# Where the experts of a graph network's last FFN are computed: inside the second attention's stream, or beside the weighted sum before it, with their outputs kept in DRAM

## The chip, the cores and the metric

One core of a Trainium2 chip runs the whole program. The metric is the device time of one execution in microseconds. A core has TensorE (PE in the profile, its weight loads are PEld), VectorE (DVE), ScalarE (ACT), GpSimd (POOL) and SyncE (SP), each with an instruction stream of its own that it executes in order; they wait for each other through semaphores. DMAs are issued from the streams of SP, ACT and POOL.

## What is computed

6250 nodes with 256 features go through four layers; each adds its output to x. `A` is the layer norm without parameters, the edge list has 206250 edges sorted by destination.

```python
x = x + gat(A(x), edges)               # attention of 4 heads x 64 over the edges
x = x + ffn0(A(x))                     # 8 experts, the best 2 per node
x = x + weighted(A(x), src, dst, w)    # sum of w * neighbour, two 256x256 matmuls, unit norm
x = x + ffn1(A(x))                     # below
```

The last layer has its own graph of 131072 edges over 8192 numbers (a second attention), which gives only the gates; its FFN has four experts, 256 to 512 to 256, and the code computes all four for every node:

```python
h = (x @ W_gat)                                     # 4 heads x 4 experts
agg = segment softmax over the edges of h           # (attention as in gat), + b_gat
s = layernorm(agg).reshape(M, 4, 4).mean(1)         # scores of the experts
w = softmax(top2(s))                                # gates g: two of four are not zero
out = sum_e g[e] * (gelu(x @ W1[e] + b1[e]) @ W2[e] + b2[e])
```

`x` inside the last layer is `A(x)` of the sum before it. The FFN's input is thus known as soon as the weighted layer has finished a node, and the gates only after the second attention.

## The kernel before

Nodes lie in 49 blocks of 128 (the last one has 106), one node per partition; X (all blocks) stays in SBUF. The edges are cut into tiles of 128, eight tiles make a piece (`Q`). Each of the three streams over edges (attention, weighted sum, second attention) works alike: GpSimd gathers the rows of the 128 sources of a tile with one indirect DMA from a table in DRAM; VectorE makes a one-hot matrix of the destinations (`one_hots`, L1092); PE multiplies it with the gathered rows and so sums them by destination in PSUM.

The program is written out in an order by hand (`manual_schedule`): Python loops over steps `s_`, and in each step emits the gathers of a piece that will be used later, and the later stages of pieces gathered in earlier steps. Every engine executes its share of that order.

**The weighted sum** (loop at L1867 to L1905, `fast`). There are 202 pieces (1612 gathers, helper at L233). In step `s_`: the gathers of piece `s_` into a tile `g1` with six buffers; the matmuls of piece `s_ - 3` (L1885), at the end of a window the copy `kept` (L1888); then the steps of a chain that a finished block goes through, one per step: `move` (L1810), `side` (transposes), `dense` (L1827 to L1832, two matmuls of 256x256 into `po`, bias, leaky ReLU), `norm` (square and square root on ACT, L1838, L1839, the addition to X, L1842), `next_ln` (the last layer's norm), `next_h` (transposes, `xT` stored to `xt_d` in DRAM, the matmul with `W_gat` into `ph`, L1855), `next_rows` (a copy and two stores, L1860 to L1862: the table of the second attention); last, the scaling of piece `s_ - 2` by the edge weights on ACT (L1903) and its one-hots on DVE.

Ahead of this loop stand its loads and, after them, the layer norms of X that write the table `tab_ef`.

**The second attention** (`layer1_fast` and `gat_stream`) begins behind a branch on a flag (`tc.If`), when all of the weighted sum is done. It has 99 pieces (787 gathers from `tab_1f`, L1199, nine buffers). A step takes the gathers of piece `s_`, the scores of piece `s_ - 2` (a matmul L1220, its reduction `nd` L1229, additions to `Z`), the greatest score per destination for four pieces together (L1245 to L1271), the messages (L1278) cut into three bf16 parts (L1283, L1285), and the sums of piece `s_ - 7` (L1301). Five times in a step it calls `beside()`, which takes one item of the list `work`.

That list holds the FFN. When the four blocks of a group have been summed, `group` loads their `xT` (`xt`, 512 KB), computes the gates (`route`) and appends the work: for each expert four `inner` items (L1624: two matmuls of 128x128 by 512 nodes; GELU on ACT, L1629), four `outer` items (L1635: four matmuls by 256; the result times its gate is added to X on DVE, L1640), and `offsets` (L1614 to L1619: the gates times `b2`). PSUM gives two buffers `pf` to these items; what follows the matmuls of an item (GELU, addition) is emitted at the next call. After the group's last item its rows of X are stored to `out`. When the loop ends, `while beside()` empties the list.

Of the kernel before, what the change touches and what calls it, by code (L numbers as in the profile page):

```python
# [31 lines left out]
P = 128  # L32
LN_EPS = 1e-5
BIG = float(2**100)
CH = 7
# [35 lines left out]
def tile_kernel(ctx, tc, src_ins, out):  # L71
# [1450 lines left out]
    def layer1_fast(s1, si1, dl1, il1, ha_d, tab_1, xt_d):  # L1522
# [3 lines left out]
        W1 = D1 + H1  # L1526
        HD = I["L1_ffn_W1"].shape[2]
        FC = HD // P
        with tc.tile_pool(name="g1f", bufs=1) as g1, tc.tile_pool(name="f1w", bufs=2) as fp, \
                tc.tile_pool(name="f1_ps", bufs=2, space=PSUM) as fpp:  # L1530
# [13 lines left out]
            w1 = g1.tile([P, E1, KD, HD], F32, name="w1")  # L1544
            nc.scalar.dma_start(w1, I["L1_ffn_W1"].rearrange("e (k p) f -> p e k f", p=P))
            w2 = g1.tile([P, E1, FC, D], F32, name="w2")
            nc.scalar.dma_start(w2, I["L1_ffn_W2"].rearrange("e (c p) d -> p e c d", p=P))
            bt = g1.tile([P, E1, FC], F32, name="bt")
            with nc.allow_non_contiguous_dma(reason="biases along the partitions"):
                nc.scalar.dma_start(bt, I["L1_ffn_b1"].rearrange("e (c p) -> p e c", p=P))  # L1550
            b2 = g1.tile([E1, D], F32, name="b2")
            nc.scalar.dma_start(b2, I["L1_ffn_b2"])
# [4 lines left out]
            ag, work, gates, xts, hs, late = {}, [], {}, {}, {}, []  # L1557
# [4 lines left out]
            def load_x(g):  # L1562
                n = len(blocks_in(g)) * P
                xts[g] = fp.tile([P, KD, GB * P], F32, name="xt")
                nc.sync.dma_start(xts[g][:, :, :n], xt_d[:, :, g * GB * P:g * GB * P + n])
# [4 lines left out]
            def done(b, acc, hs_, mp):  # L1570
                a = mp.tile([P, D1 + 2 * H1], F32, name="a24")
                nc.vector.tensor_reduce(a, acc.rearrange("p s w -> p w s"), AX.X, OP.add)
                po = mp.tile([P, H1], F32, name="po")
                nc.scalar.activation(po, a[:, W1:], AF.Exp, scale=-1.0)  # L1574
                rd = mp.tile([P, H1], F32, name="rd")
                nc.vector.scalar_tensor_tensor(rd, a[:, D1:W1], 1e-16, po, op0=OP.add, op1=OP.add)
                nc.vector.reciprocal(rd, rd)

                def hd(x):
                    return x.rearrange("p (h c) -> p h c", h=H1)  # L1580

                g = b // GB
                if g not in ag:
                    ag[g] = fp.tile([P, GB, D1], F32, name="ag")
                o = mp.tile([P, D1], F32, name="o")
                nc.vector.tensor_mul(hd(o), hd(hs_), po[:, :, None].to_broadcast([P, H1, C1]))
                nc.vector.tensor_add(o, o, a[:, :D1])
                nc.vector.tensor_mul(hd(ag[g][:, b % GB, :]), hd(o), rd[:, :, None].to_broadcast([P, H1, C1]))
                if b == blocks_in(g)[-1]:
                    group(g)  # L1590

            def group(g):

                bl = blocks_in(g)
                n = len(bl)
                N_ = n * P
                load_x(g)
                gates[g] = route(fp, ag.pop(g), n, vec)
                for e in range(E1 + 1):
                    if e < E1:  # L1600
                        for f in range(FC):
                            work.append(lambda e=e, f=f: inner(g, e, f, N_))
                    else:
                        work.append(lambda: None)
                    if e == 0:
                        work.append(lambda: offsets(g))
                    else:
                        for j in range(n):
                            work.append(lambda e=e - 1, j=j: outer(g, e, j, e == E1 - 1 and j == n - 1))

            def offsets(g):
                for j, b in enumerate(blocks_in(g)):
                    pg = fpp.tile([P, 512], F32, name="pf")
                    nc.tensor.transpose(pg[:E1, :P], gates[g][:, j, :], ident)  # L1614
                    gt = fp.tile([E1, P], F32, name="gt")
                    nc.scalar.copy(gt, pg[:E1, :P])
                    pb = fpp.tile([P, 512], F32, name="pf")
                    nc.tensor.matmul(pb[:, :D], gt, b2, start=True, stop=True)  # L1618
                    nc.vector.tensor_add(X[:, b, :], X[:, b, :], pb[:, :D])  # L1619

            def inner(g, e, f, n):
                ph = fpp.tile([P, 512], F32, name="pf")
                for k in range(KD):
                    nc.tensor.matmul(ph[:, :n], w1[:, e, k, f * P:(f + 1) * P], xts[g][:, k, :n],  # L1624
                                     start=(k == 0), stop=(k == KD - 1))

                def gelu():
                    h = hs[g, e, f] = fp.tile([P, 512], F32, name="h", bufs=2 * FC)
                    nc.scalar.activation(h[:, :n], ph[:, :n], AF.Gelu, bias=bt[:, e, f:f + 1])  # L1629
                late.append(gelu)  # L1630

            def outer(g, e, j, last):
                py = fpp.tile([P, 512], F32, name="pf")
                for f in range(FC):
                    nc.tensor.matmul(py[:, :D], hs[g, e, f][:, j * P:(j + 1) * P], w2[:, e, f, :],  # L1635
                                     start=(f == 0), stop=(f == FC - 1))
                b = g * GB + j

                def put():
                    nc.vector.scalar_tensor_tensor(X[:, b, :], py[:, :D], gates[g][:, j, e:e + 1], X[:, b, :],  # L1640
                                                   op0=OP.mult, op1=OP.add)
                    if last:
                        store(g)
                late.append(put)
# [9 lines left out]
            def beside():  # L1654
                todo = late[:]
                late.clear()
                if work:
                    work.pop(0)()
                for f in todo:
                    f()  # L1660
                return bool(work or late)
# [5 lines left out]
    def fast(flag_s0, last_d, dl_d):  # L1667
# [105 lines left out]
        xt_d = dram.tile([P, KD, NP], F32, name="xt_df")  # L1773
        with tc.tile_pool(name="n1f", bufs=1) as ep, tc.tile_pool(name="n1fw", bufs=2) as mp, \
                tc.tile_pool(name="n1f_ps", bufs=1, space=PSUM) as pp:
# [10 lines left out]
            for t0, n in chunks(NT, CH):  # L1786
                em = mp.tile([P, CH, D], F32, name="em")
                layernorm(mp, em, X[:, t0:t0 + n, :], n)
                nc.sync.dma_start(tab_e[t0 * P:(t0 + n) * P].rearrange("(t p) d -> p t d", p=P), em[:, :n])
            wg = layer1_weights(ep)  # L1790
            ips = place_iota(pp)
# [32 lines left out]
            def dense(b, eT, sT):  # L1824
                po = pp.tile([P, D], F32, name="po")
                for k in range(KD):
                    nc.tensor.matmul(po, eT[:, k], w12[:, 0, k], start=(k == 0), stop=False)  # L1827
                for k in range(KD):
                    nc.tensor.matmul(po, sT[:, k], w12[:, 1, k], start=False, stop=(k == KD - 1))
                o = mp.tile([P, D], F32, name="on")  # L1830
                nc.vector.tensor_add(o, po, bias)  # L1831
                nc.vector.scalar_tensor_tensor(o, o, 0.2, o, op0=OP.mult, op1=OP.max)  # L1832
                return o

            def norm(b, o):
                sq = mp.tile([P, D], F32, name="sq")
# [12 lines left out]
            def next_h(b, xl):  # L1849
                xT = mp.tile([P, KD, P], F32, name="xT1")  # L1850
                transposed(pp, xT, xl[:, 0, :])
                nc.sync.dma_start(xt_d[:, :, b * P:(b + 1) * P], xT)
                ph = pp.tile([P, D1 + 2 * H1], F32, name="ph1")
                for k in range(KD):
                    nc.tensor.matmul(ph, xT[:, k], wg[:, k], start=(k == 0), stop=(k == KD - 1))  # L1855
                return ph

            def next_rows(b, ph):
# [3 lines left out]
                nc.sync.dma_start(ha_d[:, b, :], h)  # L1862

            chain = {side: dense, dense: norm, norm: next_ln, next_ln: next_h, next_h: next_rows}


            with tc.manual_schedule():  # L1867
                after = {}
                s_ = 0
                while s_ < npiece + 3 or any(k >= s_ for k in after):  # L1870
                    if s_ < npiece:
                        t0, n = span(s_)
                        g = piece[s_] = mp.tile([P, Q, D], F32, name="g1", bufs=6)
# [3 lines left out]
                    if 0 <= q < npiece:  # L1877
                        t0, n = span(q)
                        g = piece.pop(q)
                        for b, a, m, oh in hots.pop(q):  # L1880
# [3 lines left out]
                            for t in range(a, a + m):  # L1884
                                nc.tensor.matmul(acc[b], oh[:, t - a], g[:, t - t0, :], start=(t == lo), stop=(t == hi))  # L1885
                            if hi == a + m - 1:
# [13 lines left out]
                    if 0 <= k < npiece:  # L1900
# [4 lines left out]
                        hots[k] = one_hots(s0, k, mp, ips, dl, 4)  # L1905
                    s_ += 1
        keep.close()
        v1 = nc.values_load(flag1[0:1, 0:1], min_val=0, max_val=1,
                            skip_runtime_bounds_check_because="a comparison: 0 or 1")
        with tc.If(v1 == 1) as cmp1:  # L1910
            layer1_fast(s1, si1, dl1, il1, ha_d, tab_1, xt_d)
# [46 lines left out]
```

## Time and profile before

| | |
|---|---|
| time, three runs | 7729.37 us median (7711.49 to 7736.43) |
| the profiled execution | 7741.2 us, span 7739.3 us |
| busy: PE / DVE / ACT / POOL | 4514.6 / 3064.3 / 1496.6 / 4066.3 us |
| TensorE's granted clock, mean | 0.773 |
| gathers of the first attention | 205 to 2535 us |
| ffn0 and the sort of the second edge list | about 2540 to 3690 us |
| gathers of the weighted sum | 3737 to 6068 us |
| gathers of the second attention | 6126 to 7555 us |
| HBM traffic | 720 MB read, 57 MB written |

The page gives each engine's busy time, then forty slices of the span with a digit for the busy share of each engine and for TensorE's granted clock, then groups of instructions by line. "x1612 | 1525.6, 946 | 907.7 <-issue" means: 1612 instructions, 1525.6 us busy, 946 ns each, 907.7 us of idle time of the engine just before them, most of it ended by its own issuing. "remote" as a releaser is a semaphore update for which the profile shows no finished instruction at that time. PE's ends are modelled. Further views that the prediction uses: busy time of each engine in chosen stretches, waits (who waited for whom, total us, times, longest), and instructions in order of time (start, us, engine, line, operation, in brackets the idle time before it and its releaser).

Three rows of the page's slices (each slice 193.5 us, digits in tenths):

```profile
PE   3355545554555679997255555555555426667668
...
POOL 0666666666666012321466666666666554555550
PEclk9677777777777689998577777777777658888888
```

### The profile page before, as it was taken

To read this page: it belongs to the slowest core of one execution; us is meant where nothing else is said; L and a number is where in the kernel's file an instruction comes from. 1 tells how busy PE (TensorE), PEld (TensorE's weight loads), DVE (VectorE), ACT (ScalarE), POOL (GpSimd) and SP (SyncE) were. 2 spreads that over 40 slices of the span, in tenths; PEclk is the share of its full clock that TensorE was granted. 3 is DMA by queue.
4 is the path that set the end of the run, shared out by engine and by line. 5 is a ranking of instruction groups with operands and counts; after the bars stand their busy time and mean duration, and the time that the engine had idled before them with its cause. 6 is when DMAs were issued, how large, how long until landed. Compare 5 with 4: busy or idle time off the path is not lost. (4 is left out here: it accounts for less than half of the span.)

```text
span 7739.3 us, 63529 instructions
## 1 busy us (share of the span) xinstructions
PE 4514.6 (58%) x19991; PEld 3428.3 (44%) x19991; DVE 3064.3 (40%) x7283; ACT 1496.6 (19%) x3742; POOL 4066.3 (53%) x4308
## 2 busy tenths in 40 slices
PE   3355545554555679997255555555555426667668
PEld 2233333433343558886144444444444314444445
DVE  4354545554544762442311211111111245555554
ACT  2000000000000112222133333333333201222222
POOL 0666666666666012321466666666666554555550
PEclk9677777777777689998577777777777658888888
DMA  4444444444444145565333333333333311111110
GB/s 132 125 120 119 121 118 118 120 120 117 120 121 118 45 131 186 188 220 173 114 92 98 99 97 97 95 96 99 96 93 98 89 28 31 36 36 31 37 36 11
DMA packets 483566, 778.20 MB, mean 101 GB/s; under 512 B 146575, under 2 KB 307759, under 8 KB 483186
## 3 DMA queue, kind: packets, MB, share of 16 engines
q0 software_dynamic: 190688, 461.74, 22.7%
q1 hardware_dynamic: 279998, 301.12, 12.9%
q10 hardware_dynamic: 12532, 11.16, 0.5%
q8 instruction: 162, 2.65, 0.1%
q14 instruction: 186, 1.52, 0.1%
HBM read 720.07 MB, written 56.78 MB: 100 GB/s over the span
## 5 line engine op out<-in xcount | busy, mean ns | idle before, releaser
L233 POOL DMA_INDIRECT g<-tab_ef,si x1612 | 1525.6, 946 | 907.7 <-issue 562.8
L1199 POOL DMA_INDIRECT g<-tab,si x1612 | 1538.7, 955 | 811.3 <-issue 516.6
L1885 PE MATMUL acc<-g,oh 128*128 128x256 f32 x3224 | 1013.5, 481 | 856.8 <-DVE oh L1092 565.8
L1885 PEld LDWEIGHTS acc<-g,oh 128*128 128x128 f32 x3224 | 784.9, 249 | 1059.1 <-ACT g L1903 574.4
L1199 POOL DMA_INDIRECT g<-tab_1f,si1s x787 | 750.5, 954 | 681.6 <-issue 570.7
L1301 PE MATMUL acc<-g,oh 128*128 128x264 f32 x3224 | 942.7, 452 | 109.4 <-DVE g L1278 60.3
L1301 PEld LDWEIGHTS acc<-g,oh 128*128 128x128 f32 x3224 | 720.9, 230 | 302.3 <-DVE g L1278 99.7
L1903 ACT ACTIVATE g<-g,wt 128x256 f32<-128x256 f32 x1612 | 663.9, 495 | 57.6 <-DMA g<-tab_ef,si 53.2
L1327 PE MATMUL bacc<-kept,wide 128*128 128x264 f32 x400 | 200.5, 652 | 648.4 <-ACT kept L1314 602.1
L1624 PE MATMUL pf<-xt,w 128*128 128x512 f32 (+1 forms) x832 | 449.1, 681 | 143.7 <-DMA xt<-xt_df 66.7
L1635 PE MATMUL pf<-w,h 128*128 128x256 f32 x1568 | 412.5, 415 | 155.5 <-DVE X L1640 103.9
L1092 DVE TENSOR_TENSOR oh<-ips,dl 128x1024 f32<-128x1024 f32 x404 | 489.1, 1211 | 0.0
L1278 DVE TENSOR_TENSOR g<-g,pe 128x2048 f32<-128x2048 f32 (+2 forms) x301 | 486.5, 1616 | 0.0
L1229 DVE TENSOR_REDUCE nd<-pd 128x64 f32<-128x192 f32 (+1 forms) x301 | 106.6, 354 | 907.8 <-remote 464.1
L1888 DVE COPY kept<-acc 128x256 f32<-128x256 f32 x101 | 42.9, 425 | 1014.9 <-remote 581.0
L1327 PEld LDWEIGHTS bacc<-kept,wide 128*128 128x128 f32 x400 | 110.7, 305 | 677.6 <-ACT kept L1314 611.3
L1635 PEld LDWEIGHTS pf<-w,h 128*128 128x128 f32 x1568 | 310.4, 206 | 220.4 <-DVE X L1640 113.7
L600 PE MATMUL ph<-xe,w 128*128 128x256 f32 x1792 | 400.9, 381 | 0.0
L613 PE MATMUL py<-w,h 128*128 128x256 f32 x1792 | 399.0, 380 | 0.0
L1831 DVE TENSOR_TENSOR on<-po,bias 128x256 f32<-128x256 f32 x49 | 20.8, 424 | 911.4 <-remote 850.9
L600 PEld LDWEIGHTS ph<-xe,w 128*128 128x128 f32 x1792 | 339.8, 191 | 45.3
L613 PEld LDWEIGHTS py<-w,h 128*128 128x128 f32 x1792 | 337.1, 191 | 43.4
(465 smaller groups left out, 5077.4 us busy)
## 6 DMA issues: line engine op xcount, KB each, us to landing
w<-in_L_ffn_W SPq DMA_DIRECT2D x112, 1024.0 KB
db<-s_d SPq DMA_DIRECT2D x299, 256.0 KB
g<-tab,si POOLq DMA_INDIRECT x1612
g<-tab_ef,si POOLq DMA_INDIRECT x1612
g<-tab_1f,si1s POOLq DMA_INDIRECT x787
yy<-tab_y SPq DMA_DIRECT2D x7, 1792.0 KB
kf<-s_keep SPq DMA_DIRECT2D x76, 96.2 KB
bb<-in_L_ffn_b SPq DMA_DIRECT2D x56, 128.0 KB
```

The costliest lines, as they stand in the source:

```text
L233: nc.gpsimd.indirect_dma_start(out=dst, out_offset=None, in_=table, in_offset=bass.IndirectOffsetOnAxis(ap=si[:, t:t + 1], axis=0))
L600: nc.tensor.matmul(ph, w1[:, k, f * P:(f + 1) * P], xe[:, k, :], start=(k == 0), stop=(k == KD - 1))
L613: nc.tensor.matmul(py, hs[f][:, i * P:(i + 1) * P], w2[:, f, :], start=(f == 0), stop=(f == FC - 1))
L1092: nc.vector.tensor_tensor(o[:, :m], ips[:, None, k * P:(k + 1) * P].to_broadcast([P, m, P]), dl[:, a:a + m, None].to_broadcast([P, m, P]), ...
L1199: nc.gpsimd.indirect_dma_start(out=g[:, j, :DH + H], out_offset=None, in_=tab, in_offset=bass.IndirectOffsetOnAxis(ap=si[:, t0 + j:t0 + j ...
L1278: nc.vector.tensor_mul(gh, gh, ps[i][:, o:o + n, :, None].to_broadcast([P, n, H, CD]))
L1301: nc.tensor.matmul(acc[b].rearrange("p s w -> p (s w)"), oh[:, t - a], m_, start=(t == lo), stop=(t == hi))
L1327: nc.tensor.matmul(sums_of[b].rearrange("p s w -> p (s w)"), shift_to(s, i, b), t, start=(i == of[0]), stop=(i == of[-1]))
L1624: nc.tensor.matmul(ph[:, :n], w1[:, e, k, f * P:(f + 1) * P], xts[g][:, k, :n], start=(k == 0), stop=(k == KD - 1))
L1635: nc.tensor.matmul(py[:, :D], hs[g, e, f][:, j * P:(j + 1) * P], w2[:, e, f, :], start=(f == 0), stop=(f == FC - 1))
L1885: nc.tensor.matmul(acc[b], oh[:, t - a], g[:, t - t0, :], start=(t == lo), stop=(t == hi))
L1903: nc.scalar.activation(piece[k][:, j, :], piece[k][:, j, :], AF.Copy, scale=wt[:, t0 + j:t0 + j + 1])
```

## The change

The FFN is taken out of the second attention and put beside the weighted sum. A new function `dense_ffn` holds its weights and its items; the weighted sum calls `beside()` behind the matmuls 1, 4 and 7 of each piece, and empties the list after its loop. `next_h` writes the transposed rows straight into the group's tile `xt` and starts a group's items when its last block has come; `xt_d` is gone. An `outer` item no longer knows a gate: DVE adds `b2` (now broadcast over the partitions) and the 128x256 result of one block and one expert goes to a new DRAM tensor `y_d` (196 stores of 128 KB). In the second attention `done` loads the four outputs of its block (`yb`, 512 KB, five buffers), and `group`'s list holds one item per block: four additions of gate times output to X on DVE. `offsets` and the FFN's weights are gone from there.

So that all of it fits: `g1` has five buffers (six before), the one-hots three (four), `sq` one (two), `po` and `ph` share the PSUM tile of the transposes, and `next_rows` is part of `next_h`. The layer norms that write `tab_ef` now stand ahead of the stream's loads, in a pool of their own.

```diff
+    def dense_ffn(e_pool, fp, fpp, y_d):
...
+        def start(g):
+            bl = range(g * GB, min(NT, (g + 1) * GB))
+            n = len(bl)
+            for e in range(E1 + 1):
+                for f in range(FC):
+                    if f == FC // 2 and e > 0:
+                        for j in range(n):
+                            work.append(lambda e=e - 1, j=j: outer(g, e, j))
+                    if e < E1:
+                        work.append(lambda e=e, f=f: inner(g, e, f, n * P))
+                    elif f < FC // 2:
+                        work.append(lambda: None)
+
+        def inner(g, e, f, n):
+            ph = fpp.tile([P, 512], F32, name="pf")
+            for k in range(KD):
+                nc.tensor.matmul(ph[:, :n], w1[:, e, k, f * P:(f + 1) * P], xts[g][:, k, :n],
+                                 start=(k == 0), stop=(k == KD - 1))
+
+            def gelu():
+                h = hs[g, e, f] = fp.tile([P, 512], F32, name="h", bufs=FC + FC // 2)
+                nc.scalar.activation(h[:, :n], ph[:, :n], AF.Gelu, bias=bt[:, e, f:f + 1])
+            late.append(gelu)
+
+        def outer(g, e, j):
+            py = fpp.tile([P, 512], F32, name="pf")
+            for f in range(FC):
+                nc.tensor.matmul(py[:, :D], hs[g, e, f][:, j * P:(j + 1) * P], w2[:, e, f, :],
+                                 start=(f == 0), stop=(f == FC - 1))
+
+            def put():
+                y = fp.tile([P, D], F32, name="y1", bufs=2)
+                nc.vector.tensor_add(y, py[:, :D], b2[:, e])
+                nc.sync.dma_start(y_d[g * GB + j, :, e, :], y)
+            late.append(put)
+
+        def beside():
+            todo = late[:]
+            late.clear()
+            if work:
+                work.pop(0)()
+            for f in todo:
+                f()
+            return bool(work or late)
...
+            def load_y(b):
+                if b < NT:
+                    ys[b] = fp.tile([P, E1, D], F32, name="yb", bufs=GB + 1)
+                    nc.sync.dma_start(ys[b], y_d[b])
...
+                load_y(b)
                 g = b // GB
...
+            def put(gates, j, b):
+                y = ys.pop(b)
+                for e in range(E1):
+                    nc.vector.scalar_tensor_tensor(X[:, b, :], y[:, e, :], gates[:, j, e:e + 1], X[:, b, :],
                                                    op0=OP.mult, op1=OP.add)
...
-                po = pp.tile([P, D], F32, name="po")
+                po = pp.tile([P, KD, P], F32, name="pt").rearrange("p k e -> p (k e)")
...
-                xT = mp.tile([P, KD, P], F32, name="xT1")
+                o = b % GB * P
+                xT = room(b // GB)[:, :, o:o + P]
                 transposed(pp, xT, xl[:, 0, :])
-                nc.sync.dma_start(xt_d[:, :, b * P:(b + 1) * P], xT)
-                ph = pp.tile([P, D1 + 2 * H1], F32, name="ph1")
+                ph = pp.tile([P, KD, P], F32, name="pt")[:, 0, :D1 + 2 * H1]
...
+                if b % GB == GB - 1 or b == NT - 1:
+                    start(b // GB)
...
-                        g = piece[s_] = mp.tile([P, Q, D], F32, name="g1", bufs=6)
+                        g = piece[s_] = mp.tile([P, Q, D], F32, name="g1", bufs=5)
...
                                 nc.tensor.matmul(acc[b], oh[:, t - a], g[:, t - t0, :], start=(t == lo), stop=(t == hi))
+                                if t - t0 in (1, 4, 7):
+                                    beside()
...
-                        hots[k] = one_hots(s0, k, mp, ips, dl, 4)
+                        hots[k] = one_hots(s0, k, mp, ips, dl, 3)
                     s_ += 1
+                while beside():
+                    pass
```

## The prediction

> **What bounds the kernel now.** I read the slices of the page first, then a table of busy time by stretch, then in two stretches the groups, the waits and the order of time. Durations are of the profiled execution: span 7739.3 us, time 7741.2; the median of the three runs shown, 7729.37, lies 12 us under it.
>
> Busy time by stretch. Columns: stretch, its length, then PE, PEld, DVE, ACT and POOL busy (instructions), PE's granted clock, DMA share, GB/s. The first row is the weighted sum's stream, first to last gather. The other three are the second attention: before its FFN begins (L1624's first matmul is at 6342.9), with the FFN, and after the last gather.
>
> ```profile
> 3737.00:6068.00 2331.00, 1247.21 (x4357) 982.04 (x4358) 406.51 (x799) 736.06 (x1905) 1525.42 (x1612) 0.73 0.34 97
> 6126.00:6330.00 204.00, 19.43 (x276) 14.97 (x276) 63.92 (x186) 5.46 (x21) 129.40 (x136) 0.50 0.26 58
> 6330.00:7555.00 1225.00, 833.85 (x4293) 510.91 (x4293) 667.70 (x2106) 268.84 (x495) 620.80 (x651) 0.84 0.18 34
> 7555.00:7739.00 184.00, 149.87 (x637) 97.40 (x637) 72.14 (x243) 46.88 (x85) 0.00 (x0) 0.90 0.04 11
> ```
>
> The reader is to see that no engine is full anywhere. In the weighted sum PE is busy 54% (1247/2331) and POOL looks 65% busy. POOL's unhindered rhythm is one gather per 1.25 us (0.95 busy, 0.30 issue, below), 10.0 us for a piece of eight. The weighted sum takes 2331/201.5 = 11.6 us per piece, the second attention 1429/98.4 = 14.5.
>
> What holds a piece beyond 10 us is seen in order of time:
>
> ```profile
> 6046.61 1.03 PE L1829 MATMUL po<-w,sT 128*128 128x256 f32 x4
> 6046.66 0.95 POOL L233 DMA_INDIRECT g<-tab_ef,si  x1 [0.30 <-issue]
> 6047.91 0.95 POOL L233 DMA_INDIRECT g<-tab_ef,si  x1 [0.30 <-issue]
> 6053.04 0.42 DVE L1831 TENSOR_TENSOR on<-po,bias 128x256 f32<-128x256 f32 x1 [18.25 <-remote]
> 6053.10 0.94 POOL L233 DMA_INDIRECT g<-tab_ef,si  x1 [4.23 <-remote]
> ```
>
> VectorE needs the sum that PE ends at 6047.64, and starts 5.4 us late, when POOL has stood still for 4 us (its ring of gathered pieces is full). From the semaphores in the trace: in 3900 to 6000 PE is idle 973 us, and for 670 of them a semaphore of PE is still to come; in 6350 to 7500 it is 152 of 355, and in ffn0 without gathers (2900 to 3600) 0 of 4. So while gathers run back to back, others learn late that PE is done. The loop PE, ACT, DVE sets the pace, and POOL waits for it. The waits of 3900 to 6000 (total us, times, longest) say the same:
>
> ```profile
> DVE on L1831 <- remote: 821.0, 40, 31.5
> DVE kept L1888 <- remote: 469.1, 35, 21.2
> POOL g L233 <- remote: 202.6, 59, 4.5
> ```
>
> **The change, part by part.** The FFN's matmuls leave the second attention for the weighted sum:
>
> ```profile
> L1624 PE MATMUL pf<-xt,w 128*128 128x512 f32 (+1 forms) x832 | 449.1, 681 | 143.7 <-DMA xt<-xt_df 66.7
> L1635 PE MATMUL pf<-w,h 128*128 128x256 f32 x1568 | 412.5, 415 | 155.5 <-DVE X L1640 103.9
> ```
>
> That is 208 + 196 items of work, 861.6 us at a granted 0.84. At full clock one costs 1.72 to 1.77 us (from 7678.7: 16 records of L1624 in 7.03 us are four items; 32 of L1635 in 7.07 us are four).
>
> *1. The weighted sum's pace (the large unknown).* A group of four blocks brings 34 entries (two empty); three are taken per piece, so 11.3 pieces of each 16.4 (201.5/49 x 4) carry FFN. PE's work in such a piece at full clock: its sixteen records, 3.62 us (6028.0), a quarter of the block's chain, (1247.2 - 992.6)/201.5 = 1.26, and three items, 5.25: together 10.1 us. Beside gathers the FFN was run at 68% busy and clock 0.84 (833.85/1225), which would make it 10.1/(0.84 x 0.68) = 17.7 us; ffn0, without gathers, is about 100% busy at 1.00: 10.1. Neither fits. The new items have a slack of one item, and the one after the piece's last matmul fills a wait that exists today; but each iteration now has ACT (GELU) and DVE (the bias addition) waiting for PE ahead of the scaling L1903 and the one-hots L1092, on which the next piece's matmuls hang. I take 80% at 0.90: 14.0 us. With 11.6 for the pieces without FFN: (11.3 x 14.0 + 5.1 x 11.6)/16.4 = 13.25, so **+1.65 x 201.5 = +333 us**. Bounds: 0 if today's idle time takes it all; 5.25 us more in each of 11.3 pieces of 16.4 if nothing overlaps: +729.
>
> The smaller edits of this stream are inside that span. Two switches to the square root and two back per block put table loads of 1283 ns (the row of L1629's ACT_TABLE_LOAD) on ACT, 5.1 us in four pieces; 208 GELUs of 0.69 add 143 us; ACT then has (736 + 143 + 251)/2664 = 42%, no bound. The 196 additions of 0.42 us and the row copy L1860, moved ahead of the one-hots, where it must wait for a matmul of its own iteration, cost DVE 82 us of its 83% idle time, plus one late PE signal per block (0 to 5.4 us, in the 14.0). Five gathered pieces for six, three one-hots for four, `po` and `ph` in the transposes' PSUM tile: a piece lives some 61 us from gather to last matmul because POOL runs ahead, not because it must; its stages need 10 + 3 + 3.3 + 10, under 5 x 10. I take nothing; 0 to +1.0 us per piece. The 196 stores (128 KB) replace the xT stores on SP; behind one that waits for DVE stand the `emb` loads, needed two iterations later. At a DMA share of 0.34 they cost nothing; without that cover one landing per block, under +100.
>
> *2. Its start.* Layer norms and table now come before the loads, and 4 MB of weights load beside the first gathers. In the second attention such loads held 340 GB/s for some 20 us. **+10** (0 to +30); POOL's ring hides part.
>
> *3. Its tail.* The last full group and the group of one block start when the loop has no slots left: 32 x 1.75 = 56 us and, as in the last rows now (7713.2 to 7735), 22: **+78** (56 to 95), all ahead of the branch to the second attention.
>
> *4. The second attention's pace.* Before its FFN begins, its scores (L1229) of pieces 5 to 14 come at 6226.5 to 6335.7, 12.1 us each; the first attention, without FFN, ran 2330/201.5 = 11.6. From there to the last score (7602.9) a piece takes 1376/94 = 14.6. I take 11.8: **-267**. Bounds: 10.0, the gathers' rhythm (-436), and 13.2, halfway to today (-135). DVE keeps four additions per block and about 7 us per piece, under either. The 49 loads of 512 KB have five buffers and are issued a group ahead: nothing; if each were late by one landing (about 5 us for xt, 53.3 us in 8 waits), +60 at most.
>
> *5. Its end.* From the last score to the end: 136.4 us, most of it FFN matmuls. Left are five iterations without gathers at DVE's 7 us, the routing and a store: 50. **-86** (-60 to -100).
>
> Sum: +333 + 10 + 78 - 267 - 86 = +68 on 7741.2, that is 7809; on the median's footing, 12 less, some **7800 us**.
>
> [...] The granted clock is 0.73 in the weighted sum, 1.00 where PE is full (the page's slices show 9) and 0.50 where it has little to do (6126 to 6330). [...]
>
> **The rivals.**
>
> *A, faster: the FFN disappears in PE's idle time.* The weighted sum has 2331 - 1247 = 1084 us of it, the work at full clock is 404 x 1.75 = 707. For it: PE's idle time is mostly waiting for late signals, during which independent matmuls may run, and a busier PE is clocked higher. Against: PE executes in order, so two of a piece's three items stand between its matmuls and delay the last. FFN pieces at 12.1, average 11.95: +70; then +70 + 10 + 78 - 267 - 86 = -195: 7535. It decides at an average of 12.9 us per piece: (353 - 88)/201.5 = 1.3 over today.
>
> *B, the forecast: shared.* 7800.
>
> *C, much slower: items add serially.* Late signals reach the two PSUM buffers of the items, PE stalls in front of an item, and FFN pieces take 16.0: average 14.6, +605; sum +340, 8070. For it: DVE's waits above, up to 31.5 us long. Against: in the second attention the same two buffers lost only 152 us to late signals.
>
> *D, no difference:* the two streams' terms cancel within 0.3%, about what a measurement of this kernel tells from no change.
>
> That the FFN does not move is excluded by the instruction order of the changed program: its matmuls stand between those of the pieces.
>
> **How the numbers follow.** A 0.34, B 0.41, C 0.19, D 0.06. Faster by over 0.3%: A, 0.34. Within: D, 0.06. Slower: B and C, 0.60. B's own range: 7755 to 7950. The whole range goes from A with half of term 4's further gain (7520) to C's middle with its later half left out (8120): the bounds added up would reach 7330 and 8400, and I leave out one in ten at each end.
>
> **What would show it.** Right: the weighted sum's gathers last 2600 to 2750 us with PE over 75% busy at a clock of 0.85 to 0.95, some 80 us of FFN matmuls with POOL idle follow, and the second attention's gathers take 1130 to 1200 us with PE under 20% busy at about 0.50. Wrong: gathers of the weighted sum in under 2550 us (A), or over 2850 (C); a second attention that still takes 13 us per piece without its FFN (the late signals, not the FFN, were its bound); waits of SP or DVE for `y1` or of PE for `pf` at the head of the list, which I priced at little.

## The result, and the profile after

The changed kernel takes **7764.21 us** (median of 5 runs, 7755.07 to 7785.47) against 7729.37 (5 runs of the kernel before, 7709.21 to 7736.43): ratio 1.0054, 95% interval 1.0031 to 1.0078, half a per cent or 35 us slower. The profiled execution took 7785.47 us with a span of 7783.7, against 7741.2 and 7739.3.

Busy time by stretch of the changed kernel, columns as in the prediction's first table: the weighted sum's gathers, the tail up to the second attention's first gather, the second attention from its fifth score to its last, and the end.

```profile
3734.00:6241.00 2507.00, 1754.65 (x6407) 1305.09 (x6408) 478.40 (x976) 985.68 (x2186) 1530.56 (x1612) 0.84 0.35 99
6241.00:6391.00 150.00, 125.64 (x500) 90.96 (x498) 27.15 (x70) 40.57 (x90) 0.54 (x2) 0.92 0.12 36
6492.00:7730.00 1238.00, 181.47 (x2529) 145.35 (x2530) 741.37 (x2298) 79.33 (x258) 692.12 (x715) 0.50 0.23 52
7730.00:7784.00 54.00, 6.08 (x68) 5.11 (x67) 40.65 (x153) 7.62 (x15) 0.00 (x0) 0.50 0.08 23
```

The reader is to see the two streams beside each other. With the FFN in it the weighted sum has PE 70% busy (1754.65/2507) at a clock of 0.84. The second attention is left with a PE that is 15% busy at 0.50, and still needs 1238/94 = 13.2 us per piece. By the prediction's terms (profiles of before and after, us):

| term | before | after | measured | predicted |
|---|---|---|---|---|
| 1 weighted sum, first to last gather | 2330.0 (11.56 per piece) | 2506.2 (12.44) | +176 | +333 |
| 2 its first gather comes at | 3736.8 | 3734.2 | -3 | +10 |
| 3 last gather to the next stream's first | 58.8 | 151.0 | +92 | +78 |
| 4 second attention, fifth score to last | 1376 (14.64) | 1237 (13.16) | -139 | -267 |
| 5 last score to the end | 136.5 | 53.7 | -83 | -86 |
| sum | | | +44 | +68 |

The FFN's groups of matmuls, which before stood beside the second attention (columns: group, count, then busy us and mean ns, then idle time just before):

```profile
L1571 PE MATMUL pf<-w,h 128*128 128x256 f32 x1568 | 408.5, 409 | 38.4 <-ACT h L1565 38.4
...
L1560 PE MATMUL pf<-xt,w 128*128 128x512 f32 (+1 forms) x832 | 399.6, 609 | 0.6
```

They cost 808 us of PE (861.6 before) and PE waits only 39 us for their inputs (299 before): an item is ready whenever PE comes to it. What waits is behind them. The waits of the weighted sum, 4000 to 6240 (total us, times, longest):

```profile
ACT h L1565 <- PE pf L1560: 377.7, 86, 12.3
DVE on L1848 <- PE pt L1846: 314.9, 29, 14.6
DVE y L1576 <- PE pf L1571: 296.8, 98, 5.3
...
DVE kept L1906 <- remote: 243.2, 14, 21.5
```

The new work of ACT and VectorE (L1565, L1576) now waits for PE's items; the old waits for a late sum ("remote", 821 and 469 us in the same places before) have shrunk to 243 and less. By the semaphores, PE is idle 849 us in the weighted sum, and for 382 of these a semaphore of PE is still to come (before: 1188 and 753). These figures, here and in what follows, count a gap of PE whole in the stretch in which it ends, so the first gap, ahead of the first piece, is in them; between the first and the last gather alone PE is idle 752 us (before: 1084), with the same 382 and 753.

Only PE's signals are late. In the profile of before, from 3737 to 6068, all 493 records of VectorE's semaphore and all 854 of ScalarE's lie within 0.1 us of the end of one of that engine's instructions; of PE's 1731 records, 853 come more than 1 us after the last signalling matmul that ended ahead of them (none of 2746 in the changed kernel's weighted sum on a chip without late signals, a0 below).

The second attention shows where its 13.2 us go, in order of time:

```profile
6656.35 0.94 PE L1301 MATMUL acc<-s,oh 128*128 128x72 bf16 x13 [7.05 <-issue]
...
6667.69 0.94 POOL L1199 DMA_INDIRECT g<-tab_1f,si1s  x1 [0.30 <-issue]
6671.43 0.36 DVE L1229 TENSOR_REDUCE nd<-pd 128x64 f32<-128x192 f32 x1 [15.13 <-remote]
...
6678.97 0.94 POOL L1199 DMA_INDIRECT g<-tab_1f,si1s  x1 [10.34 <-issue]
```

PE has nothing to do after 6657.3. Its semaphores of that time come singly at 6660.87, 6668.57, 6669.27, 6671.37 and 6671.40, and then eight more within 0.3 us (6672.09 to 6672.37); POOL's last gather ended at 6668.6. VectorE starts at 6671.43, after 15 us of waiting, and POOL, whose ring is full by then, stands still for 10.3 us. Of PE's 1074 us of idle time from the fifth score to the last, a semaphore is still to come in 465. There are no FFN matmuls here any more.

### The profile page after: what moved, and what is told of

Its sections match the earlier page's. It is cut to its first block, busy times and chain, and to the rows that moved or that the text cites. A ratio compares the mean times of both kernels' runs of the same rounds, so it can differ in the third digit from the quotient of the medians.

```text
span 7783.7 us, 63729 instructions
## 1 busy us (share of the span) xinstructions
PE 4292.4 (55%) x19844; PEld 3340.5 (43%) x19844; DVE 3136.3 (40%) x7430; ACT 1535.1 (20%) x3735; POOL 4085.4 (52%) x4308
## 5 line engine op out<-in xcount | busy, mean ns | idle before, releaser
L1901 PE MATMUL acc<-g,oh 128*128 128x256 f32 x3224 | 902.3, 427 | 596.3 <-DVE oh L1092 244.7
L1901 PEld LDWEIGHTS acc<-g,oh 128*128 128x128 f32 x3224 | 679.9, 216 | 808.4 <-issue 467.0
L1301 PEld LDWEIGHTS acc<-g,oh 128*128 128x128 f32 x3224 | 716.8, 228 | 295.2 <-DVE g L1278 114.6
L1301 PE MATMUL acc<-s,oh 128*128 128x72 bf16 x1267 | 96.7, 251 | 615.0 <-DVE s L1283 439.6
L1571 PE MATMUL pf<-w,h 128*128 128x256 f32 x1568 | 408.5, 409 | 38.4 <-ACT h L1565 38.4
L1560 PE MATMUL pf<-xt,w 128*128 128x512 f32 (+1 forms) x832 | 399.6, 609 | 0.6
L1301 PEld LDWEIGHTS <-oh 128*128 128x128 bf16 x1267 | 90.2, 134 | 618.8 <-issue 553.3
```

Source lines behind the costliest of these rows:

```text
L1301: nc.tensor.matmul(acc[b].rearrange("p s w -> p (s w)"), oh[:, t - a], m_, start=(t == lo), stop=(t == hi))
```

## The experiments

Theory 1: signals of PE that come late beside the gathers bound both streams; the FFN filled such waits in the weighted sum, and taking it out of the second attention leaves the waits there. Theory 2: the loop's own work (VectorE's chain, additions, loads) bounds the second attention. The experiments of one group share a chip; the chip differs from group to group, and this turned out to matter more than the change (the kernel before took 7729.37, 7832.92, 6790.38 and 6788.74 us). The profiles of the chip of the first group, on which the changed kernel itself was not run:

| kernel | weighted sum, us (per piece) | PE idle, of it a semaphore to come | to next stream | score to score | idle, to come |
|---|---|---|---|---|---|
| e1, no FFN | 2389.8 (11.86) | 1259, 753 | 54.9 | 13.65 | 1118, 650 |
| e4, its matmuls alone | 2450.4 (12.16) | 803, 314 | 147.5 | 13.63 | 1110, 636 |
| e2, changed, extra matmuls in second attention | 2526.6 (12.54) | 876, 404 | 150.6 | 14.39 | 637, 193 |
| e3, changed, 7 gathered pieces in second attention | 2563.8 (12.72) | 905, 421 | 150.5 | 13.57 | 1089, 474 |

**e1_no_ffn.**

```diff
-                if b % GB == GB - 1 or b == NT - 1:
-                    start(b // GB)
...
-                load_y(b)
...
-                y = ys.pop(b)
-                for e in range(E1):
-                    nc.vector.scalar_tensor_tensor(X[:, b, :], y[:, e, :], gates[:, j, e:e + 1], X[:, b, :],
-                                                   op0=OP.mult, op1=OP.add)
```

> The changed kernel without the last FFN: no item is ever queued in the weighted sum, and the second attention neither loads stored outputs nor adds them (its output lacks the last FFN). All the small edits stay (5 gathered pieces, 3 one-hots, shared PSUM tile, norms ahead of the loads). Theory 1 (late PE signals bound the second attention once its FFN is gone): scores still every 12.7 to 13.2 us, total second attention within 50 us of the changed kernel's 1315. Theory 2 (the loads of 512 KB and the four additions per block bound it): scores every 12.0 us or less, at least 110 us less. For the weighted sum: if the small edits cost nothing, its gathers take 2310 to 2350 us as before (11.6 per piece); if they are part of the 176 us that it grew, more than 2370. Total under theory 1: 7785 - 176 - 85 = 7500 to 7540.

7633.2 us, 0.9751 (0.9723 to 0.9779) of the kernel before, which takes 7832.92 us on this chip; the 7500 to 7540 were reckoned from the first chip's 7785. Scores come every 13.65 us without FFN, loads and additions (theory 1 expected 12.7 to 13.2): these are not the second attention's bound, and that part of theory 2 falls. The weighted sum's 2389.8 is over the 2370 that was set as a sign; this chip is some 0.9% slower beside gathers (the first attention, the same in all kernels, takes 11.76 us per piece here and 11.66 on the other), so that by estimate 40 of its 60 us are the small edits, 0.2 us per piece. That is little more than what one stream differs by from profile to profile: the same weighted sum takes 2526.6, 2537.5 and 2563.8 us in e2, e6 and e3 on this chip.

**e4_matmuls_only.**

```diff
-            late.append(gelu)
...
-                nc.tensor.matmul(py[:, :D], hs[g, e, f][:, j * P:(j + 1) * P], w2[:, e, f, :],
+                nc.tensor.matmul(py[:, :D], w1[:, e, 0, f * P:(f + 1) * P], w2[:, e, f, :],
-            late.append(put)
...
-                load_y(b)
```

> The changed kernel with the FFN's matmuls alone in the weighted sum: no GELU on ACT, no bias addition, no store, and no loads and additions in the second attention (its output lacks the last FFN; the second product takes weights in place of the GELU's result). If PE's time is what lengthens the weighted sum (the step of the prediction's term 1), its gathers keep 2450 to 2510 us; if ACT's and VectorE's waits for PE ahead of the scaling and the one-hots do it, they fall back to 2310 to 2400.

7809.2 us, 0.9976 (0.9957 to 0.9996). The matmuls add 61 us to the weighted sum and 93 to what follows it (2450.4 and 147.5 against 2389.8 and 54.9); the GELUs, additions and stores add another 76 to 113 (2526.6 and 2563.8 in e2 and e3, whose weighted sum is that of the changed kernel). The 2450.4 lie at the lower edge of the first branch of the expectation, but that stream without any FFN takes 2389.8 here and with all of it over 2526: both halves count. Which is the larger is not secure, since e2 and e3 run the same stream and differ by 37 us. The idle time of PE shrinks by 456 us, 439 of them time in which a semaphore was to come: most of the FFN's matmuls ran while late signals were on their way.

**e2_extra_second.**

```diff
+                for k in range(1):
+                    nc.tensor.matmul(extra, ident, dl[:, :512], start=True, stop=True)
                 if work:
                     work.pop(0)()
```

> The changed kernel with one idle 128x128 by 128x512 matmul at each of the five places per iteration of the second attention where its gate additions are queued; the product is never read. Some 5 x 0.9 = 4.4 us of PE work per piece at full clock. Theory 1 (an almost idle PE at a clock of 0.50 signals late, a busy one promptly): scores every 12.0 us or less, so 110 us or more are gained, clock above 0.50. Theory 2 (the pace is set by the handshakes and VectorE's work, whatever PE does in between): 13.2 to 14.6 us per piece, 0 to 130 us lost.

7948.77 us, 1.0145 (1.0119 to 1.0172). The line of its second attention:

```profile
6480.00:7830.00 1350.00, 694.54 (x3362) 318.42 (x3363) 700.50 (x2169) 74.37 (x245) 703.84 (x734) 0.72 0.21 46
```

PE is 51% busy and its clock 0.72 in place of 0.50, and a piece takes 14.39 us, 0.8 more than with the idle PE on the same chip. That a busier PE at a higher clock is heard sooner does not hold: VectorE's reductions `nd` still wait 401 us in sum beyond the end of their product, against 296 to 303 in e1, e3 and e4. (The smaller idle time with a semaphore to come, 193, says nothing here: the extra matmuls stand in it.) It also bears on why the FFN cost time in the second attention: matmuls without any use beyond their own time, 694 us busy in place of 181, cost 0.8 us per piece, about half of the 1.5 that the FFN's leaving saved on the first chip.

**e3_seven_gathered.**

```diff
-                g = piece[q] = mp.tile([P, Q, W], F32, name="g", bufs=9)
+                g = piece[q] = mp.tile([P, Q, W], F32, name="g", bufs=7 if parts == 3 else 9)
```

> The changed kernel with 7 gathered pieces in the second attention's ring in place of 9: POOL can run ahead of the loop less. If PE's signals come late because POOL issues gathers back to back for long stretches, POOL now pauses in every iteration and the signals come sooner: 13.2 us per piece or less. If the ring only smooths (the lateness has another cause), POOL's waits come on top: 13.5 to 15 us per piece, 30 to 170 us lost.

7854.83 us, 1.0021 (1.0005 to 1.0037). 13.57 us per piece and 474 us against 13.63 to 13.65 and 636 to 650 in e1 and e4: two pieces less of lead change nothing that can be told. A ring shorter than seven was not tried.

**The next group, on another chip: b0_before_again, a0_after_again, e6_rest_carried, e7_ffn_beside_second.**

> The kernel before once more, for its stages beside those of the experiments on their chip: weighted sum's gathers 2330 to 2370 us, scores of the second attention every 14.5 to 15.0 us.

> The changed kernel once more, beside its variants on the same chip: 1.002 to 1.008 of the kernel before; weighted sum's gathers 2500 to 2570 us, 150 us from their last to the next stream's first, scores every 13.1 to 13.7 us.

Both expectations fail, by far more than anything in this study: the kernel before takes **6790.38 us** here (7 runs, 6785.74 to 6792.69), 12% less than in the comparison above, and the changed one 6723.62, **0.9904** (0.9887 to 0.9920): one per cent faster. First the kernel before, weighted sum and second attention, then the changed kernel, the same four stretches as above:

```profile
3414.00:5431.00 2017.00, 1475.28 (x4450) 976.35 (x4451) 413.67 (x816) 878.49 (x1937) 1526.31 (x1611) 0.79 0.39 112
5503.00:6651.00 1148.00, 835.04 (x4700) 519.31 (x4699) 748.54 (x2333) 285.81 (x538) 721.46 (x753) 0.85 0.21 40
```

```profile
3405.00:5501.00 2096.00, 1708.78 (x6406) 1259.29 (x6407) 479.67 (x976) 997.06 (x2186) 1525.81 (x1612) 0.91 0.42 118
5501.00:5653.00 152.00, 127.91 (x501) 92.44 (x499) 27.15 (x70) 40.88 (x90) 0.90 (x2) 0.92 0.11 35
5697.00:6667.00 970.00, 182.25 (x2542) 145.73 (x2539) 739.98 (x2296) 79.32 (x258) 733.22 (x753) 0.50 0.30 68
6667.00:6721.00 54.00, 6.07 (x68) 5.11 (x67) 41.02 (x154) 7.62 (x15) 0.00 (x0) 0.50 0.08 23
```

Single instructions last about as long as before (a gather of the weighted sum 948 ns against 946, the scaling L1903 506 against 495), but in no stretch is a semaphore of PE to come while PE is idle (0 of 646 us and 0 of 313 before, 0 of 484 and 0 of 783 after). The weighted sum runs at POOL's rhythm of 10.01 us per piece, and so does the first attention (10.10). The stage without gathers back to back (from the first attention's last gather to the weighted sum's first) takes 1197 us, against 1206: what differs is the signals beside gathers, and not the transfers, whose time is alike (software queue 25.5% of 6787.7, 1731 us; before 22.7% of 7739.3, 1757). The change's terms on this chip: weighted sum +79 (10.01 to 10.40 per piece), tail +125 (27.7 to 152.4), second attention -178 (12.21 to 10.32, now near POOL's rhythm), end -83, start -9; sum -66, measured -67 between the spans.

**e5_sync_loads**, on the chip of e1 to e4 again, together with the second run of e6.

```diff
-                            gather(g[:, j, :], tab_e, si, t0 + j)
+                            o = (t0 + j) % NT * P
+                            nc.sync.dma_start(g[:, j, :], tab_e[o:o + P])
...
+                    if parts == 3:
+                        o = (t0 + j) % NT * P
+                        nc.sync.dma_start(g[:, j, :DH + H], tab[o:o + P])
+                        continue
```

> The changed kernel with GpSimd's gathers of the weighted sum and of the second attention replaced by plain transfers of the same size that SyncE issues: 128 rows in a row of the table in place of 128 gathered ones (so both streams sum wrong rows). First attention unchanged. On a chip where PE's signals come late beside gathers: if the gathers that GpSimd issues are the cause, PE's idle time with a semaphore still to come falls from 382 and 465 us in the two streams to under 50, and both streams fall under 10.0 us per piece; if the transfers themselves (their bytes and packets) are the cause, it stays above 200 and the pace above 11. On a chip without late signals, the pace in both is under 10.0 us, since no POOL rhythm binds any more.

6830.56 us, one run, against 7833.66 of the kernel before. Three stretches: the first attention with POOL's gathers, the weighted sum and the second attention without.

```profile
182.00:2548.00 2366.00, 1199.84 (x5322) 906.65 (x5323) 1147.48 (x2047) 110.02 (x486) 1536.47 (x1612) 0.72 0.45 119
3714.00:5797.00 2083.00, 1680.32 (x6450) 1258.71 (x6451) 514.12 (x1107) 988.81 (x2207) 0.00 (x0) 0.92 0.41 122
5959.00:6775.00 816.00, 182.39 (x2546) 145.79 (x2544) 722.94 (x2298) 79.26 (x258) 0.00 (x0) 0.50 0.33 81
```

In one execution, PE is idle 1174 us in the first attention with a semaphore to come in 766 of them, and 461 and 629 us in the two streams with none. The waits of the weighted sum in this run name only engines that had really just ended, as

```profile
DVE kept L1911 <- PE acc L1906: 431.8, 99, 16.4
```

while its first attention still has waits for nothing that the profile can name:

```profile
ACT kept L1318 <- remote: 768.1, 38, 21.5
```

So the gathers that POOL issues hold PE's signals on this chip, and transfers of the same bytes from SyncE do not. Which part of a gather does it is not separated: e5 changes the issuing engine, the queue and the addresses (rows in a row in place of scattered ones) at once. It is not the number of packets, which rises: the two streams' 219.5 MB go in 345 thousand packets where the gathers' took 103 thousand. Without the gathers the second attention takes 8.67 us per piece with PE 22% busy at a clock of 0.50, and the weighted sum with the FFN 10.34 (the expected "under 10.0" held for one of the two). The step from 13.6 (e3, on this chip) to 8.67 has two parts, the signals and POOL's rhythm; the other chip, where the rhythm alone is left, has 10.32.

**e6_rest_carried** (two chips): what is left of the FFN after the last piece goes to the second attention's places.

```diff
-                while beside():
-                    pass
...
+                more = rest()
                 if work:
```

> The changed kernel, but the items that are left after the last piece of the weighted sum are not run out ahead of the branch: they are run beside the second attention's first pieces, one per place (its rings: 8 gathered pieces for 9, 4 loaded outputs for 5). If the tail is pure loss, as term 3 of the prediction has it, the gap between the streams falls from 150 to 55 us, some 65 items are done in the first 14 pieces of the second attention for 0 to 20 us, and the total falls by 75 to 95 us, to 0.992 to 0.996 of the kernel before. If the start of the second attention hides something else in that gap, less than 50 us are gained.

> The kernel with the rest of the FFN carried into the second attention, once more. Where signals come late: 75 to 100 us less than the changed kernel, 0.993 to 0.997 of the kernel before. Where they do not: 0.9853 as measured.

Without late signals 6690.73 us, 0.9853 (0.9836 to 0.9869): better than both kernels. The gap falls from 152.4 to 78.4 us, 41 are given back before the fifth score and 5 at the end; 33 remain (6723.62 to 6690.73), less than half of the expectation and in its second branch, under 50: the tail is not pure loss. With late signals 7888.65 us, 1.0066 (1.0042 to 1.0090): the gap falls by 75 there too (150.5 to 75.5), but the first five scores take 147 us (80 to 110 in e1 to e4) and the later ones 13.75 each. Expected were 0.993 to 0.997. Work that moves into a stream with late signals is not free even where PE is 15% busy, as e2 showed (14.39 us per piece for e3's 13.57). The changed kernel itself was not run on this chip; e3, its nearest, took 7854.83 us.

**e7_ffn_beside_second** (two chips): the FFN beside the second attention as before, but ahead of the gates.

```diff
-                                if t - t0 in (1, 4, 7):
-                                    beside()
...
+            room, start, dense = dense_ffn(g1, fp, fpp, y_d)
...
+                rest()
                 if work:
```

> The changed kernel with all the FFN's items back beside the second attention, but still ahead of the gates, through the stored outputs; the weighted sum has none (its xT goes through DRAM again). Theory 1 (the FFN fills PE's waits in both streams and what counts is the work that hangs behind the last piece): no tail and no end work, 7833 - 83 plus 30 to 60 for the small edits = 0.990 to 0.998 of the kernel before. Theory 2 (VectorE's chain sets the second attention's pace): its additions, now two sets of 196, come on top, 15.0 us per piece or more, 1.000 to 1.010 of the kernel before.

> The kernel with all the FFN beside the second attention and ahead of the gates, once more. Where signals come late: the weighted sum as without FFN (11.8 to 11.9 us per piece, 50 more than the kernel before), scores every 14.6 to 15.2 us, no tail, 54 us after the last score: 7834 + 50 - 83 + 0 to 60 = 0.996 to 1.004 of the kernel before. Where they do not: 0.988 as measured.

0.9880 (0.9864 to 0.9897), and 0.9879 (0.9862 to 0.9895) on a third chip, again one without late signals (0 in every stretch). Theory 1's 0.990 to 0.998 was reckoned with 7833 us and late signals, theory 2's 15.0 us per piece did not come. The weighted sum is back at 10.01 us per piece, the gap at 34 us, the end at 53.8, and a piece of the second attention takes 11.94, less than the 12.21 of the kernel before in spite of 196 more additions. So the end's 83 us are won without moving the FFN to the other stream; the change's own way (0.9904) moves more and wins less. What e7 does where signals come late was not seen.

**e10_spaced_gathers**, on the third chip.

```diff
+                    if parts == 3:
+                        nc.gpsimd.memset(pause, 0.0)
```

> The changed kernel with a memset of 128 x 248 (0.29 us) on POOL after each gather of the second attention, so that gathers follow each other every 1.55 us in place of 1.25 and a piece's take 12.4 us. Where signals come late: if it takes gathers back to back to hold the signals, PE's idle time with a semaphore to come falls from 465 us to under 150 and scores come every 12.4 to 12.8 us; if any gather in progress holds them, it stays above 300 and scores come every 13.3 us or more. Where they do not come late: 12.4 to 12.6 us per piece against 10.3.

6867.04 us, 1.0113 (1.0096 to 1.0130). Scores come every 11.76 us, below the expected 12.4 to 12.6: a gather follows the last after 1.465 us (1151.5/786), since the memset of 0.34 us partly takes the place of the 0.30 us of issue (POOL's idle time before a gather is 138.3/787 = 0.18 beside it). POOL's rhythm sets the second attention's pace where signals are prompt: 0.19 us more per gather (1.279 in a0) is 1.5 per piece, and 1.44 were measured. Whether spacing helps late signals stays open, since this chip has none.

## Why the prediction came out as it did

It said 7800, slower, and 7764 was measured: inside forecast B's own range (7755 to 7950), and the direction is right, but the change is half of the one forecast (+35 for +71). That the sum came so near is luck: two large terms missed, by -157 and +128, and cancelled. The direction is luck too in so far as it holds only where signals come late; without late signals the kernel was one per cent faster.

*The bound.* Right, and more than the prediction knew: late signals of PE set the pace of both streams there. e5 shows it in one run on another chip with late signals, and the two chips without them give the size: 7729 against 6790 us.

*Step 1, the weighted sum's pace (+333, measured +176).* The failing step is "I take 80% at 0.90: 14.0 us". Part of it is arithmetic: the pace was charged for all groups, while the last full group and the group of one block were charged again in step 3; with eleven groups 125 pieces carry items, not 139, which is some 33 us (14 x 2.4). The rest is the size: (2506.2 - 76.5 x 11.57)/125 = 13.0 us for a piece with FFN. What made it smaller is rival A's mechanism: the matmuls alone cost 61 us (e4 against e1), since they ran while signals were on their way (382 us of such idle time for 753). The prediction gave that to A and not to the forecast. Other idle time takes them in as well: without late signals the stream grew by only 79 us. What the forecast held against A, matmuls between those of a piece, was not the only cost: the GELUs and additions on ACT and VectorE, priced as no bound at 42% of ACT, cost 76 to 113 us, at least as much as PE's time as far as two profiles tell. The small edits, "I take nothing; 0 to +1.0", are about 0.2 us per piece by estimate, which is near what profiles of one stream differ by.

A's own condition, an average under 12.9 us per piece, was met at 12.44. The kernel still came out slower, because step 4 failed too.

*Step 2 (+10, measured -3).* The loads and their issue hold ACT: those of `bt` and `b` (L1534, L1536) occupy its queue for 12.60 and 7.94 us, and the scaling starts only at 3759.4, 25 us after the first gather (2.8 before). The gathers' ring takes it up: up to 3900 POOL's waits other than issue are 16.8 us (16.0 before).

*Step 3 (+78, measured +92).* Right, inside its bounds (56 to 95). On the chip with prompt signals it is 125, because the gap before was shorter (27.7 us for 58.8; with the change 152.4 for 151.0).

*Step 4, the second attention's pace (-267, measured -139).* The step that failed is the choice of 11.8 from pieces 5 to 14. The changed kernel runs those pieces in 12.2 us, as the kernel before did (12.1), and pieces 25 to 84 in 13.3 each: the opening is not the stream's steady pace. Why it is faster here is not shown; without late signals it is slower (10.9 against 10.1). The measured 13.16 is the bound that the prediction gave (13.2), and its sign of being wrong ("a second attention that still takes 13 us per piece without its FFN (the late signals, not the FFN, were its bound)") came true. Without late signals the other bound (10.0) is nearly met, 10.32.

*Step 5 (-86, measured -83).* Right, on both chips where both kernels ran (136.5 and 136.6 to 53.7).

*The clock.* Most of the stretches looked at agree in direction: PE was granted 0.50 in the changed kernel's second attention with 15% busy, 0.73 in the weighted sum of before with 54%, 0.84 in the changed one with 70%, 0.92 in e5's with 81%, 1.00 in ffn0 (before, 2900 to 3600) with 99%; the weighted sum of b0, 0.79 with 73%, stands out of that order. In the profile of before the 592 single records of the clock are 0.50 or 1.00 and nothing else, so these are means. The 0.90 that the forecast took for the pieces with FFN was the author's estimate, between the 0.84 of the FFN beside gathers and ffn0's 1.00; 0.84 is what the whole weighted sum with FFN was granted. But the clock was not what decided: e2 raised it from 0.50 to 0.72, and a piece took 14.39 us for e3's 13.57.

*The signs.* Most of the forecast's own signs missed: the weighted sum took 2506 us for 2600 to 2750, with PE 70% busy at 0.84 for over 75% at 0.85 to 0.95, and the second attention's gathers 1308 us for 1130 to 1200. Weighted sum under 2550 us was named as rival A's sign, and it came; the tail and a PE under 20% at 0.50 came as said. Waits of PE for `pf` did not come (0.6 and 38.4 us before the items); what heads the list are waits of ACT and VectorE for PE's `pf` (377.7 and 296.8 us).

Open: why POOL's gathers hold PE's signals on one chip and not on others. That every chip that shows 7700 to 7850 us for the kernel before has late signals, and both with 6790 have none, is seen; what makes a chip one or the other is not. One chip was seen late at two times; the two prompt ones were seen at one time each, so that the chip decides, and not the hour, is not shown either. And since the profile models the ends of matmuls, whether a matmul itself ends late or only its signal is not told apart; PE goes on meanwhile: in the profile of before no signal of it comes from 6041.35 to 6046.27, while seven matmuls that give one end by the profile and another matmul starts every 0.2 to 0.4 us.

## What to carry to other kernels

Before pricing a move of work between stages, see what the receiving and the giving stage wait for: idle time that is a wait for a late signal takes independent matmuls in cheaply, though not for nothing (61 us in e4; in e2 some 510 us of them cost 75), and the same wait stays behind as the bound when the matmuls go (13.16 us per piece here). Take a stage's pace without the work from its steady part, not from its opening, and count an item either in a pace or in a tail. Work that does not depend on what the stage computes (here the experts' outputs) is worth starting early above all because it then leaves the stage's end: that is 83 us here, wherever the FFN stands.

## What the runs showed of the hardware that was not expected

- One program takes 7729 to 7834 us on some chips and 6789 to 6790 on others; the runs on one chip agree within 0.8%. The difference lies in the streams with POOL's gathers: 11.66 to 11.76 us per piece in the first attention against 10.10 (b0).
- On the slower kind, semaphores of PE arrive up to 15 us after the matmul, in the place shown above, while POOL issues gathers of 0.95 us every 1.25 us. In the same execution on the same chip (e5) there were no late ones in two streams whose transfers SyncE issued (766 us of PE's idle time with a signal to come, then 0 and 0).
- The sign of the change depends on it: 1.0054 with late signals, 0.9904 without. Each was measured on one chip.
- POOL's memset of 128 x 248 between two gathers takes 0.34 us and delays the next gather by 0.19 (e10: 1.465 us from gather to gather, 1.279 in a0).
